# Deformable convolution on one core: chunks of consecutive window positions, with only the tokens that reach them

## The chip, the cores and the metric

One Trainium2 chip, one of its cores. The metric is the device time of one execution in microseconds; three runs of the kernel before are given with their median. The profile is of one more execution. Engine names: PE is the matrix engine (TensorE; its weight loads are listed apart, as PEld), DVE is VectorE, ACT is ScalarE, POOL is GpSimd, and SP is the engine from whose queue this kernel issues its transfers.

## The reference, cut to what matters

The network has four layers over eight images of 56 x 56 positions and 128 channels. Layers 0, 2 and 3 are of one kind, a deformable convolution (DCN) with a multilayer perceptron behind it; layer 1 is a state-space scan and isn't touched here. Of a DCN layer:

```python
xp = x @ w_in + b_in
h = gelu(batchnorm(depthwise_conv3x3(x)))
offset = (h @ w_off + b_off).reshape(N, H, W, GROUP, P, 2)
mask = softmax((h @ w_msk + b_msk).reshape(N, H, W, GROUP, P))
y = dcn_core(xp, offset, mask) @ w_out + b_out
x = x + gamma1 * layer_norm(y, ln1_g, ln1_b)
m = gelu(x @ w_fc1 + b_fc1) @ w_fc2 + b_fc2
x = x + gamma2 * layer_norm(m, ln2_g, ln2_b)
```

dcn_core takes, for every token, for each of 4 channel groups of 32 and each of 9 taps, a bilinear sample of xp at the tap's place plus its offset, and adds the 9 samples with the mask's weights. All is float32.

## The kernel before

**From gathering to matrix products.** The kernel doesn't gather. A block is 14 rows by 8 columns of an image: 112 tokens (TB). All samples of a token fall into a window of WY rows around it, and the windows of a block's tokens lie in one rectangle of 14 + WY - 1 rows, each PC positions wide. The weights of a token's 36 samples are added up into its own window, as one row of numbers per channel group. Shifted so that all 112 rows refer to the same rectangle, these rows are a matrix `sw` [112 tokens, 4 groups, SLEN positions]. The result of a group is then this matrix times the rectangle's rows of xp, `xw` [positions, 128 channels]. Row r of a block's tokens has nonzero weights in the rectangle's rows r to r + WY - 1 only; the rest of its row of `sw` is zeros.

**Chunks.** [...] the rectangle is cut into NJ chunks of KP positions. Stage 0 (layer 0): WY 14, PC 18, 4 chunks of 128. Stage 2: WY 12, PC 17, 4 of 112. Stage 3: WY 15, PC 21, 5 of 120. Before, chunk j holds the positions j, j + NJ, j + 2 NJ, ...: the positions are dealt out to the chunks in turn, so each chunk reaches over the whole rectangle.

**A block's work** (`sample`, lines 725 to 736, and `products`, lines 738 to 741). For each chunk: four PE transposes (line 732), one a group, turn the chunk's columns of `sw`, [112, KP] with a stride of NJ elements, into [KP, 112] in a PSUM bank `pt`; one ACT copy (line 734) brings the 4 x 112 columns to `st` in SBUF; four matrix products (line 741), one a group, with the chunk's rows of `xw` as the stationary operand (KP x 32), add [32, 112] into the block's columns of `yps`. Each float32 product is two instructions in the trace, a transpose is one. The products stand two chunks behind the transposes (`LAG`). A chunk's first product starts the sum, the last chunk's ends it.

**Loading.** `fetch` (lines 715 to 723) issues two transfers a block from SP's queue, two blocks ahead, into tiles with three buffers: `sw` from a table in DRAM to which `weigh` has stored the tokens' windows, and `xw` from the table that holds xp cut into strips. `windows` gives the second one's address pattern; before, partition p takes the NJ positions from p x NJ on, which lie side by side, so a partition's part is one contiguous piece of NJ x 512 bytes.

**The order around it** (`loop`, lines 826 to 875). Blocks run image by image, 4 block rows of 7 blocks: 224 a stage. Between the blocks' work the loop deals out, step by step, the tail of the block row before (output projection, two layer norms, the perceptron), the front of the next image (projection, depthwise convolution, offsets and masks) and `weigh`, which runs 6 blocks ahead (DVE adds each tap's patch into a window that POOL has cleared; ACT makes the bilinear weights). Each engine runs its instructions in the order that the framework's scheduler has written out; transfers leave SP's queue in theirs. Stores are collected and issued behind a fetch (`flush`).

Of the kernel before, what the change touches and what calls it, by code (L numbers as in the profile page):

```python
# [41 lines left out]
F32 = mybir.dt.float32  # L42
# [18 lines left out]
BR, BC = 14, 8  # L61
TB, NCB, NRB = BR * BC, W // BC, H // BR
# [12 lines left out]
class Geo:  # L75


    def __init__(self, y0, wy, x0, wx, kx, ky):
        self.Y0, self.WY, self.X0, self.WX = y0, wy, x0, wx

        self.PC, self.HR = BC + wx - 1, 14 * -(-(H + wy - 1) // 14)
        m = (BR + wy - 1) * self.PC
        self.NJ = -(-m // 128)
        self.KP = 8 * -(-m // self.NJ // 8)
        if self.KP % 16 and self.KP != 120:
            self.KP += 8
        self.SLEN = self.NJ * self.KP

        self.SA = G * self.SLEN
        self.WPAD = -(-(wy * self.PC + wx - kx) // 4) * 4  # L90


G, NP, CG = 4, 9, 32
# [363 lines left out]
class Dcn:  # L457
# [207 lines left out]
    def windows(self, i, c, rb=None):  # L665

        t, geo = self.table[i % 3], self.geo
        at = geo.HR * geo.PC * c
        if rb is None:
            return t[at : at + geo.HR * geo.PC].rearrange("(r x) c -> r (x c)", x=geo.PC)  # L670
        at += BR * rb * geo.PC
        return t[at : at + geo.SLEN].rearrange("(p j) c -> p (j c)", j=geo.NJ)

# [39 lines left out]
    def fetch(self, i, rb, q):  # L715

        nc, n, geo = self.nc, TB, self.geo
        sw = self.bp.tile([128, G, geo.SLEN], F32, name="sw", tag="sw")
        nc.sync.dma_start(out=sw[:n].rearrange("p g m -> p (g m)"), in_=self.slot(NRB * i + rb, q=q))
        xw = self.bp.tile([128, geo.NJ, C], F32, name="xw", tag="xw")  # L720
        last = nc.sync.dma_start(out=xw[: geo.KP].rearrange("p j c -> p (j c)"), in_=self.windows(i, q, rb))
        self.here[i, rb, q] = sw, xw
        return last

    def sample(self, i, rb, q, yps):

        nc, n, KP, NJ = self.nc, TB, self.geo.KP, self.geo.NJ
        sw, xw = self.here.pop((i, rb, q))
        for j in range(NJ):
            ps = self.pt.tile([128, 512], F32, name="pt", tag="pt")  # L730
            for g in range(G):
                last = nc.tensor.transpose(ps[:KP, n * g : n * (g + 1)], sw[:n, g, j::NJ], self.net.ident[:n, :n])  # L732
            st = self.bp.tile([128, G * n], F32, name="st", tag="st", bufs=4)
            nc.scalar.copy(st[:KP], ps[:KP, : G * n])  # L734
            self.behind.append(partial(self.products, yps, xw, st, j))
            self.catch_up(LAG, last)

    def products(self, yps, xw, st, j):
        n, KP = TB, self.geo.KP
        for g in range(G):  # L740
            self.nc.tensor.matmul(yps[CG * g : CG * (g + 1), :], lhsT=xw[:KP, j, CG * g : CG * (g + 1)], rhs=st[:KP, n * g : n * (g + 1)], start=j == 0, stop=j == self.geo.NJ - 1)  # L741

    def catch_up(self, lag, last=None):
        while len(self.behind) > lag:
# [692 lines left out]
```

## Time and profile before

| | |
|---|---|
| median of 3 runs | 19078.62 us (19069.39 to 19079.6) |
| profiled execution | 19113.06 us, span 19111.5 us |
| PE | busy 14938.0 us, 78% of the span |
| DVE | 15302.6 us, 80% |
| ACT | 11472.3 us, 60% |
| POOL | 11709.1 us, 61% |
| transposes, L732 | x11648, 2271.6 us busy, mean 327 ns |
| copies, L734 | x2912, 1516.3 us, 541 ns |
| products, L741 | x23296, 1357.6 us, 308 ns |
| granted PE clock | mean 0.833 |
| DMA, the three DCN loops | 0.84, 0.78 and 0.74 busy |

How to read it: the span's busy shares mix very different stages. The three DCN stages take about the first 2.3 ms and the last 5 ms; the scan layer with its long DVE and POOL instructions lies between them. A matrix instruction's length in the trace [...] overlaps with the next ones, so the distance from one start to the next tells more than the mean. PE's clock is granted in two values, half and full[...]. A line number is that of the kernel before.

### The profile page before, as it was taken

How to read it: one execution, taken by the hardware profiler on the slowest of the kernel's cores; microseconds unless marked ns; L12 is line 12 of the kernel's file. 1: busy time of each engine (PE TensorE's matmuls, PEld its weight loads, DVE VectorE, ACT ScalarE, POOL GpSimd, SP SyncE). 2: the span in 40 equal slices, each digit the busy share in tenths (PEclk: the TensorE clock that was granted, in tenths of full speed). 3: DMA queues.
4: the chain of work that ended last, by engine and by line, in shares of the span. 5: the costliest groups of instructions: out<-in, count | busy, mean ns of one | idle time of the engine just before them, and what ended most of it. 6: DMA issues, size and time to landing. Idle time of an engine off the chain costs nothing. (4 is left out here: it accounts for less than half of the span.)

```text
span 19111.5 us, 237768 instructions
## 1 busy us (share of the span) xinstructions
PE 14938.0 (78%) x80131; PEld 7162.2 (37%) x80131; DVE 15302.6 (80%) x18773; ACT 11472.3 (60%) x21363; POOL 11709.1 (61%) x6462
## 2 busy tenths in 40 slices
PE   5988877678778778778778778777667999588888
PEld 3666522122222222222222222222135666455555
DVE  6777468988988988988889889888957776677775
ACT  3666655566656556566556566656555666456565
POOL 1111069989989989988989989988951111111111
PEclk7888888889888888888888888888877888677777
DMA  8888633344443433344344443443326878577776
GB/s 240 230 222 228 185 127 139 138 142 143 141 143 140 144 141 140 141 142 144 138 143 142 143 143 138 146 144 130 138 88 187 214 211 207 154 205 203 195 205 173
DMA packets 981448, 3112.21 MB, mean 163 GB/s; under 512 B 76320, under 2 KB 518452, under 8 KB 912380
## 3 DMA queue, kind: packets, MB, share of 16 engines
q1 hardware_dynamic: 980204, 3096.75, 52.3%
q8 instruction: 644, 10.55, 0.2%
q14 instruction: 600, 4.92, 0.1%
HBM read 2395.38 MB, written 872.17 MB: 171 GB/s over the span
## 5 line engine op out<-in xcount | busy, mean ns | idle before, releaser
L1349 POOL TENSOR_TENSOR hc<-h,bc 128x784 f32<-128x784 f32 x4096 | 7568.1, 1872 | 1034.4 <-DVE h L1344 791.0
L1344 DVE TENSOR_TENSOR_SCAN h<-dA,st,u 128x784 f32<-128x784 f32 x3072 | 5577.7, 1837 | 392.0 <-ACT dA L1246 256.9
L1246 ACT ACTIVATE dA<-dt,v_A 128x784 f32<-128x784 f32 x4096 | 3741.2, 914 | 785.3 <-DVE h L1344 782.1
L1278 PE MATMUL acc<-hc,v_sum 128*32 128x392 f32 x16384 | 3422.7, 566 | 92.6 <-POOL hc L1349 92.1
L1256 DVE TENSOR_TENSOR u<-dtu,bc 128x784 f32<-128x784 f32 x3072 | 2883.1, 956 | 596.0 <-PE dtu L1240 468.9
L1240 PE MATMUL dtu<-dt,ident 128*128 128x392 f32 x4096 | 2103.4, 640 | 1342.2 <-issue 937.2
L732 PE MATMUL pt<-ident,sw 112*120 112x112 f32 (+2 forms) x11648 | 2271.6, 327 | 260.7 <-DMA sw<-skew 254.6
L734 ACT COPY st<-pt 120x448 f32<-120x448 f32 (+2 forms) x2912 | 1516.3, 541 | 1408.6 <-PE pt L732 1396.0
L700 POOL MEMSET win<- 128x1820 f32 (+2 forms) x384 | 631.5, 1647 | 2768.7 <-DMA skew<-win 2273.6
L1344 DVE TENSOR_TENSOR_SCAN h<-dA,st,up 128x784 f32<-128x784 f32 x1024 | 1878.8, 1835 | 258.9 <-POOL hc L1349 133.3
L732 PEld LDWEIGHTS pt<-ident,sw 112*120 112x120 f32 (+2 forms) x11648 | 1672.4, 204 | 852.4 <-issue 733.9
L1347 ACT COPY st<-h 128x1 f32<-128x1 f32 x3072 | 580.1, 189 | 2254.7 <-DVE h L1344 2244.6
L1252 POOL TENSOR_TENSOR up<-dt,bc 128x784 f32<-128x784 f32 x1024 | 1899.7, 1855 | 35.6 <-DVE h L1344 30.7
L1278 PEld LDWEIGHTS acc<-hc,v_sum 128*32 128x32 f32 x16384 | 804.4, 120 | 2617.4 <-issue 1702.9
L1240 PEld LDWEIGHTS dtu<-dt,ident 128*128 128x128 f32 x4096 | 858.7, 233 | 2417.8 <-issue 1481.9
L709 DVE TENSOR_TENSOR win<-win,patch 112x252 f32 (+2 forms) x3456 | 1558.2, 462 | 58.1 <-issue 17.3
L706 DVE TENSOR_TENSOR patch<-ay,hat 112x756 f32<-112x756 f32 (+2 forms) x1152 | 1213.2, 1065 | 488.5 <-POOL ay L697 488.4
L697 POOL TENSOR_TENSOR ay<-hat,om 112x756 f32<-112x756 f32 (+2 forms) x192 | 398.9, 2078 | 1950.8 <-ACT hat L693 1633.4
L741 PE MATMUL yps<-st,xw 120*32 120x112 f32 (+2 forms) x23296 | 1357.6, 308 | 133.8 <-ACT st L734 128.7
L1023 PE MATMUL misc<-xn,v_tap 128*128 128x448 f32 x2016 | 875.4, 579 | 120.3 <-ACT xn L1057 63.5
L1289 ACT COPY y<-acc 64x392 f32<-64x392 f32 x768 | 576.2, 750 | 460.4 <-PE acc L1278 450.4
L595 DVE SCALAR_TENSOR_TENSOR cv<-pad,w_col,cv 128x784 f32<-128x784 f32 x768 | 798.5, 1040 | 4.7
(158 smaller groups left out, 19403.2 us busy)
## 6 DMA issues: line engine op xcount, KB each, us to landing
dt<-dds SPq DMA_DIRECT2D x1024, 784.0 KB
bc<-rows SPq DMA_DIRECT2D x512, 784.0 KB
sw<-skew SPq DMA_DIRECT2D x224, 1050.0 KB
sw<-skew SPq DMA_DIRECT2D x224, 896.0 KB
dds<-dd SPq DMA_DIRECT2D x256, 784.0 KB
sw<-skew SPq DMA_DIRECT2D x224, 784.0 KB
skew<-win SPq DMA_DIRECT2D x128, 964.7 KB
skew<-win SPq DMA_DIRECT2D x128, 771.8 KB
```

What stands on the lines that cost most here:

```text
L706: nc.vector.tensor_mul(patch[:n], bcast(a, 3, KX), bcast(b, 2, KY))
L709: self.last_add = nc.vector.tensor_add(to, to, patch[:n, NCB * p : NCB * (p + 1)]).ins
L732: last = nc.tensor.transpose(ps[:KP, n * g : n * (g + 1)], sw[:n, g, j::NJ], self.net.ident[:n, :n])
L734: nc.scalar.copy(st[:KP], ps[:KP, : G * n])
L741: self.nc.tensor.matmul(yps[CG * g : CG * (g + 1), :], lhsT=xw[:KP, j, CG * g : CG * (g + 1)], rhs=st[:KP, n * g : n * (g + 1)], start=j = ...
L1240: last = nc.tensor.matmul(ps[:, b, :SH], lhsT=self.net.ident, rhs=s["dt", cg][:, 1, SH * b : SH * (b + 1)], start=True, stop=True)
L1246: nc.scalar.activation(da[:, :SC], s["dt", cg][:, 0], AF.Exp, scale=w["A"][:, k, NSG * cg + sg : NSG * cg + sg + 1])
L1252: nc.gpsimd.tensor_mul(u, s["dt", cg][:, 1], s["bc", sg][:, 0])
L1256: nc.vector.tensor_mul(halves[0], s["dtu", cg][:, :, :SH], halves[1])
L1278: nc.tensor.matmul(acc[r : r + TC, :SH], lhsT=w["sum"], rhs=hc[:, SH * b : SH * (b + 1)], start=False, stop=sg == NSG - 1)
L1344: nc.vector.tensor_tensor_scan(hh[:, ::step], dA[:, :SC][:, ::step], u[:, ::step], st[:, t : t + 1], ALU.mult, ALU.add)
L1349: nc.gpsimd.tensor_mul(hc, hh, s["bc", sg][:, 1])
```

## The change

Chunk j now holds the KP consecutive positions from j x KP on. Only some of the rectangle's rows fall into it, and so only tokens of some block rows have weights there. A new list `chunks` in the geometry gives for each chunk its number and the tokens t0 to t1 that can reach it; t0 is either 0 or 64. They are sorted so that a chunk with all 112 tokens comes first, since it starts the sum over all columns. In order, the chunks cover: stage 0 tokens 0 to 112, 0 to 112, 0 to 64 and 64 to 112; stage 2 0 to 112, 0 to 112, 0 to 56 and 64 to 112; stage 3 0 to 112 twice, 0 to 96, 0 to 48 and 64 to 112. Transposes, copy and products of a chunk work on these tokens alone. The transposes' source is now contiguous (no stride), and where a chunk has 64 tokens or fewer, they use half of PE's rows, the lower or the upper half. In `xw`, partition p now holds the positions p, KP + p, 2 KP + p, ..., so a partition's part comes in NJ pieces of 512 bytes. The numbers of instructions and of transfers stay as they are.

```diff
@@ class Geo
+        self.chunks = []
+        for j in range(self.NJ):
+            top, last = j * self.KP // self.PC, ((j + 1) * self.KP - 1) // self.PC
+            t0, t1 = BC * max(0, top - wy + 1), BC * min(BR, last + 1)
+            self.chunks.append((j, 64 if t0 >= 64 else 0, t1))
+        self.chunks.sort(key=lambda chunk: (chunk[1], -chunk[2]))
+        assert self.chunks[0][1:] == (0, TB)
@@ def windows
-        return t[at : at + geo.SLEN].rearrange("(p j) c -> p (j c)", j=geo.NJ)
+        return t[at : at + geo.SLEN].rearrange("(j p) c -> p j c", j=geo.NJ)
@@ def fetch
-        last = nc.sync.dma_start(out=xw[: geo.KP].rearrange("p j c -> p (j c)"), in_=self.windows(i, q, rb))
+        last = nc.sync.dma_start(out=xw[: geo.KP], in_=self.windows(i, q, rb))
@@ def sample
-        nc, n, KP, NJ = self.nc, TB, self.geo.KP, self.geo.NJ
+        nc, KP = self.nc, self.geo.KP
         sw, xw = self.here.pop((i, rb, q))
-        for j in range(NJ):
+        for at, (j, t0, t1) in enumerate(self.geo.chunks):
+            n = t1 - t0
             ps = self.pt.tile([128, 512], F32, name="pt", tag="pt")
             for g in range(G):
-                last = nc.tensor.transpose(ps[:KP, n * g : n * (g + 1)], sw[:n, g, j::NJ], self.net.ident[:n, :n])
-            st = self.bp.tile([128, G * n], F32, name="st", tag="st", bufs=4)
-            nc.scalar.copy(st[:KP], ps[:KP, : G * n])
-            self.behind.append(partial(self.products, yps, xw, st, j))
+                last = nc.tensor.transpose(ps[:KP, n * g : n * (g + 1)], sw[t0:t1, g, KP * j : KP * (j + 1)], self.net.ident[t0:t1, t0:t1])
+            st = self.bp.tile([128, G * TB], F32, name="st", tag="st", bufs=4)
+            nc.scalar.copy(st[:KP, : G * n], ps[:KP, : G * n])
+            self.behind.append(partial(self.products, yps, xw, st, at))
             self.catch_up(LAG, last)
@@ def products
-    def products(self, yps, xw, st, j):
-        n, KP = TB, self.geo.KP
+    def products(self, yps, xw, st, at):
+        KP = self.geo.KP
+        j, t0, t1 = self.geo.chunks[at]
+        n = t1 - t0
         for g in range(G):
-            self.nc.tensor.matmul(yps[CG * g : CG * (g + 1), :], lhsT=xw[:KP, j, CG * g : CG * (g + 1)], rhs=st[:KP, n * g : n * (g + 1)], start=j == 0, stop=j == self.geo.NJ - 1)
+            self.nc.tensor.matmul(yps[CG * g : CG * (g + 1), t0:t1], lhsT=xw[:KP, j, CG * g : CG * (g + 1)], rhs=st[:KP, n * g : n * (g + 1)], start=at == 0, stop=at == self.geo.NJ - 1)
```

## The prediction

> **What bounds the kernel now.** I read the sliced page first, to find where the changed code runs: the three deformable-convolution (DCN) stages, slices 0 to 4 and 30 to 39; the 12 ms between them are another layer, which the diff doesn't touch. Then each DCN loop as one window (stage 0, 2, 3 in turn; columns: window, length, then busy us and instructions of PE, PE's weight loads, DVE, ACT and POOL, granted PE clock, DMA share, GB/s), then who PE and the DMA queue wait for.
>
> ```profile
> 260.00:2260.00 2000.00, 1779.26 (x14710) 1242.62 (x14708) 1424.74 (x3120) 1285.19 (x2442) 361.30 (x204) 0.84 0.84 228
> 14480.00:16320.00 1840.00, 1695.86 (x14696) 1177.88 (x14694) 1262.37 (x3108) 1233.17 (x2381) 308.67 (x203) 0.88 0.78 207
> 16550.00:19075.00 2525.00, 2133.77 (x17360) 1432.22 (x17355) 1844.92 (x3123) 1529.92 (x2843) 428.58 (x203) 0.77 0.74 201
> ...
> SPq L721 <- PE yps L741: 676.4, 151, 22.0
> PE pt L732 <- DMA sw<-skew: 69.1, 33, 7.7
> ```
>
> PE is busy 89, 92 and 85% of the loops; DVE, ACT and POOL have more room. In stage 0 the queue that loads a block's data waits 676 us for PE to free a buffer, and PE waits only 69 us for that data. So PE sets the pace, with DMA close behind (0.84 in stage 0). Clocks of 0.84, 0.88 and 0.77, between the values 0.5 and 1.0 that the records hold, mean half clock for 32, 24 and 46% of the time.
>
> What PE does per chunk shows in the timeline (start, length, instruction, count): two chunks at full clock in stage 0, one at half clock in stage 2, and transposes of the same form whose source lies contiguous (L562, L776), at full clock.
>
> ```profile
> 1043.98 0.73 PE L732 MATMUL pt<-ident,sw 112*128 112x112 f32 x4
> 1044.64 0.40 PE L741 MATMUL yps<-st,xw 128*32 128x112 f32 x8
> 1044.97 0.73 PE L732 MATMUL pt<-ident,sw 112*128 112x112 f32 x4
> ...
> 14500.72 0.60 PE L741 MATMUL yps<-st,xw 112*32 112x112 f32 x8
> 14501.26 1.01 PE L732 MATMUL pt<-ident,sw 112*112 112x112 f32 x4
> 14502.20 0.60 PE L741 MATMUL yps<-st,xw 112*32 112x112 f32 x8
> ...
> 14510.52 0.68 PE L732 MATMUL pt<-ident,sw 112*112 112x112 f32 x4
> 14620.63 0.55 PE L562 MATMUL ps<-ident,xt 112*128 112x112 f32 x4
> 15138.04 0.60 PE L776 MATMUL ps<-ident,X 112*128 112x112 f32 x4 [0.27 <-DVE X L823]
> ```
>
> A chunk takes 0.99 us at full clock (1043.98 to 1044.97) and 1.48 at half. A block has 4, 4 and 5 chunks, 224 blocks a stage; 7080 product instructions in the first window, 32 a block, make 221 blocks in 2000 us: 9.05 us a block. The others likewise: 8.33 and 11.41.
>
> **Part 1, fewer columns.** From the geometry, chunks cover (112, 112, 64, 48), (112, 112, 56, 48) and (112, 112, 96, 48, 48) tokens instead of 112 each: 112, 120 and 144 columns less a block. The price of a column comes from start-to-start times in the trace: L783 with 448 columns starts every 376 ns at full clock, 747 at half: 0.84 and 1.67 ns. A token is streamed by 4 transposes one after another, and by 8 product instructions that run as 2 rounds of four side by side (starts 6 ns apart within a round, 100 between rounds): 6 column times, 5.0 and 10.0 ns. Per block: 0.56, 0.60, 0.72 us at full clock, 1.12, 1.20, 1.44 at half.
>
> [...] contiguous transposes (L776, 128 columns) start 96 ns apart, and their loads, when pulled ahead, as little as 57. [...]
>
> **Part 2, contiguous source.** Four transposes of strided `sw` take 0.73 us (128 positions), 0.68 (112); contiguous ones 0.60 with the switch ahead, 0.55 without. I take 0.13 a chunk in stage 0 and 0.08 in 2 and 3: 0.52, 0.32, 0.40 us a block. At half clock both forms start 187 ns apart: nothing.
>
> In the measured clock mix: stage 0 0.68x1.08 + 0.32x1.12 = 1.09 us; stage 2 0.76x0.92 + 0.24x1.20 = 0.99; stage 3 0.54x1.12 + 0.46x1.44 = 1.27. Times 224: 750 us of PE time.
>
> **Part 3, the 64-row mode.** Chunks of 64 tokens or fewer use transposes on half the rows. [...] 190 to 213 ns between a product and a transpose against 96 to 120 between two transposes. But every chunk already changes mode twice; the built instruction order has 11,592 changes against 11,424. 168 more at 0.1 us each: 17 us. No transpose on 64 rows is in this trace; bounds in the rivals.
>
> **Part 4, copies.** L734 takes 541 ns for 448 columns and L563's 336 take 438: 0.92 ns a column, so ACT loses about 0.4 us a block. It lies beside PE; without that cover (a product that waits for its copy, 36, 22 and 71 us in the loops) it is a small gain. Counted as nothing.
>
> **Part 5, the `xw` load.** Same bytes, but 512 B pieces instead of 2048 or 2560 B, 4 or 5 times as many. In the trace's packet records a 2048 B packet takes 130 ns in stage 0 (84 when undisturbed), 512 B packets in the middle layer 28. So 512 B costs 28, or by the same crowding 28x130/84 = 44; I take 36. Stage 0: 128 x 130 / 16 engines = 1.04 us a block becomes 512 x 36 / 16 = 1.15; stage 2 0.95 becomes 1.0, stage 3 1.11 becomes 1.35. Issuing costs little: `skew<-win` with 784 pieces takes 352 ns on SP, `xw` now 333. Waits are not added; behind this load stand the stores and the next `sw`, two blocks ahead of PE.
>
> **The sum.** DMA is busy 7.6, 6.5 and 8.4 us a block, then 7.7, 6.6, 8.6. The best half millisecond holds 0.85; I allow 0.90 (4 us windows reach 0.95): at least 8.55, 7.3 and 9.6 us. So stage 0 gains 0.5 of its 1.09; 2 and 3 are not capped. There I let three quarters through, since PE sits 8 and 15% idle on others and a less busy PE is granted less clock (0.88 at 92% busy, 0.77 at 85%): 0.74 and 0.95. (0.5 + 0.74 + 0.95) x 224 = 491, less 12 for the modes = 479. Profiled execution 19,113 (span 19,111.5): 18,634; the median of the runs lies 34 lower, so **18,600**.
>
> **Rivals.**
> - *PE alone sets it:* all 733 us come through: 18,346. For it: the queue's 676 us behind PE. Against: DMA would have to hold 0.97 in stage 0.
> - *Small pieces cost 55 ns:* DMA grows by 0.72, 0.59, 0.95 us a block; at 0.90 the blocks change by +0.15, -0.43, -0.95: 18,805.
> - *64-row transposes are no shorter:* only products, stride and copies gain, 372 us, some 70% through: 18,820. For it: no such row; against: L1001's 98 columns start 84 ns apart, 112 take 96.
> - *PE time turns into idle and lower clock:* no change, about 19,060.
> - *Slower, by the small pieces:* the place is `xw` at L721. At 80 ns a piece DMA grows by 1.5, 1.3, 1.9 us a block, and at 0.90 the blocks end at 10.1, 8.66, 11.4: +310 us, 19,389. It decides from about 67 ns, where the three stages cancel. Against it stand the 28 ns, and `skew<-win`'s 1008 B pieces at 55 ns in stage 0 itself.
>
> **Chances.** Forecast 0.49 (its own range 18,450 to 18,750), PE alone 0.12, 55 ns pieces 0.13, no shorter 0.08, no change 0.06, slower 0.12. Faster by over 0.2% (38 us, about what a measurement here can tell): 0.82; same 0.06; slower 0.12. The range 18,330 to 19,010 leaves out the slower case, no change, and a sliver below.
>
> **What would show it.** Right: L732's small forms start some 50 to 60 ns apart at full clock and 80 to 110 at half; four full ones take 0.60; a block takes 8.5, 7.6 and 10.4 us; 512 B packets 28 to 44 ns; DMA share up, to about 0.9 in stage 0. Wrong: small forms at 96 or 187 ns; PE waiting for `sw` or `xw` well over 69 us in stage 0; PE's clock falling to 0.7 with PE less busy and blocks as long as now. The middle layer should keep its length; if it doesn't, something that I haven't priced moved.

## The result: 0.3% faster, where 2.5% was forecast

| | before | after |
|---|---|---|
| median of 8 runs each | 19088.15 us (19069.39 to 19109.13) | 19028.97 us (19011.1 to 19048.64) |
| profiled execution | 19113.06 us | 19048.64 us |
| granted PE clock, mean | 0.833 | 0.805 |
| PE busy, whole span | 14938.0 us | 14638.0 us |

The ratio is 0.9966, 95% interval 0.9957 to 0.9976. The forecast was 18,600, its range 18,330 to 19,010.

**The profile after.** The three DCN loops as windows (window, length, busy us and instructions of PE, PE's weight loads, DVE, ACT and POOL, granted PE clock, DMA share, GB/s):

```profile
260.00:2220.00 1960.00, 1669.05 (x14566) 1135.37 (x14569) 1423.20 (x3092) 1189.44 (x2412) 365.01 (x203) 0.75 0.87 229
14460.00:16270.00 1810.00, 1620.88 (x14571) 1098.67 (x14564) 1262.82 (x3096) 1146.37 (x2352) 306.49 (x204) 0.78 0.81 211
16500.00:19010.00 2510.00, 2022.53 (x17540) 1364.21 (x17540) 1859.74 (x3143) 1431.99 (x2865) 433.67 (x206) 0.70 0.78 205
```

The clock stood at 0.84, 0.88 and 0.77 before; it is 0.75, 0.78 and 0.70 now. The page's clock row, in 40 slices, shows where: first before, then after.

```profile
PEclk7888888889888888888888888888877888677777
```

```profile
PEclk7777788889888888888888888888776777676677
```

Slices 1 to 4, 28, 30 to 33, 36 and 37 (counted from 0) go down by a tenth; from 5 to 27, most of which is the middle layer, the row is unchanged. That layer kept its length: from the last `yT` of stage 0 to the first of stage 2 it is 12,234 us before and 12,242 after. From one copy of `yT` to the next, a block takes 8.90, 8.23 and 11.22 us, against 8.99, 8.27 and 11.39 by the same measure before: 0.09 + 0.04 + 0.17 = 0.30 us, times 224 blocks 67 us. That is the whole difference between the two profiled executions (64 us).

The changed lines themselves did shrink, by the page's groups (busy us, mean ns, then idle time ahead of them and its releaser):

```profile
L741 PE MATMUL pt<-ident,sw 112*128 112x112 f32 (+8 forms) x11648 | 1901.3, 300 | 354.3 <-DMA sw<-skew 348.4
L743 ACT COPY st<-pt 128x448 f32<-128x448 f32 (+6 forms) x2912 | 1236.7, 443 | 1359.5 <-PE pt L741 1312.7
L752 PE MATMUL yps<-st,xw 120*32 120x48 f32 (+8 forms) x23296 | 1211.8, 294 | 213.0 <-ACT st L743 197.8
```

Transposes lost 2271.6 - 1901.3 = 370 us and products 1357.6 - 1211.8 = 146, together 516. But PE as a whole lost 300 only. Its other instructions, the same 45,187 in both kernels, are busy 179 us longer, all of it in the three loops (their records added up by themselves: 2551 us before, 2731 after); the rest of the difference is overlap. And of these 300 the span got 64; what remains became idle time. Waits in stage 0 after (us in total, times, longest), the queue's and PE's:

```profile
SPq L540 <- DVE win L717: 464.6, 76, 13.9
SPq L729 <- PE pt L741: 406.6, 102, 17.8
SPq L729 <- PE yps L752: 214.8, 62, 10.5
...
PE pt L741 <- DMA sw<-skew: 93.3, 44, 6.7
PE yps L752 <- ACT st L743: 63.6, 34, 6.7
```

The first line before:

```profile
SPq L532 <- DVE win L709: 384.1, 74, 11.6
```

At the load of `xw` the queue still waits for PE to free buffers (406.6 + 214.8 = 621 us; before 676.4 + 37.0 = 713 by the same view). But the first line, which the prediction left out, is as long: before it can issue the stores of `weigh`, the queue waits for DVE to finish the windows. In stage 3 that is its longest wait in both kernels (722.9 us before, 801.0 after). So PE paces the blocks, but not alone; DVE stands close behind it. PE itself waits more for `sw` (93 us, 69 before) and for copies (64, 33 before by the same view).

One place of stage 3 shows both the gain and its price (timeline of PE after; start, length, instruction, count, idle before):

```profile
16728.79 0.43 PE L741 MATMUL pt<-ident,sw 48*120 48x48 f32 x4
...
16729.84 0.37 PE L752 MATMUL yps<-st,xw 120*32 120x96 f32 x8
16733.77 0.57 PE L741 MATMUL pt<-ident,sw 112*120 112x112 f32 x4 [3.55 <-DMA sw<-skew]
...
16734.58 1.00 PE L741 MATMUL pt<-ident,sw 112*120 112x112 f32 x4
16735.52 0.39 PE L752 MATMUL yps<-st,xw 120*32 120x48 f32 x8
...
16737.20 0.63 PE L741 MATMUL pt<-ident,sw 48*120 48x48 f32 x4
```

At 16728.79 a chunk of 48 tokens needs 0.43 us for its transposes. Then PE waits 3.55 us for `sw`, finds full clock for one more chunk's transposes (the clock record falls to half at 16734.2), and from 16734.58 on everything takes its half-clock length: the same 48 tokens 0.63 us.

### The profile page after: what moved, and what is told of

It reads as the page before. It is cut to its first block, busy times and chain, and to the rows that moved or that the text cites. A ratio compares the mean times of both kernels' runs of the same rounds, so it can differ in the third digit from the quotient of the medians.

```text
span 19047.1 us, 237826 instructions
## 1 busy us (share of the span) xinstructions
PE 14638.0 (77%) x80131; PEld 6918.2 (36%) x80131; DVE 15315.5 (80%) x18773; ACT 11199.2 (59%) x21363; POOL 11707.3 (61%) x6462
## 5 line engine op out<-in xcount | busy, mean ns | idle before, releaser
L741 PE MATMUL pt<-ident,sw 112*128 112x112 f32 (+8 forms) x11648 | 1901.3, 300 | 354.3 <-DMA sw<-skew 348.4
L743 ACT COPY st<-pt 128x448 f32<-128x448 f32 (+6 forms) x2912 | 1236.7, 443 | 1359.5 <-PE pt L741 1312.7
L741 PEld LDWEIGHTS pt<-ident,sw 112*128 112x128 f32 (+8 forms) x11648 | 1329.5, 170 | 879.1 <-issue 647.4
L752 PE MATMUL yps<-st,xw 120*32 120x48 f32 (+8 forms) x23296 | 1211.8, 294 | 213.0 <-ACT st L743 197.8
L794 PE MATMUL ps<-xT,w_fc 128*128 128x448 f32 (+1 forms) x1536 | 794.0, 651 | 114.8 <-ACT xT L789 86.9
```

The source lines that it names most:

```text
L743: nc.scalar.copy(st[:KP, : G * n], ps[:KP, : G * n])
L752: self.nc.tensor.matmul(yps[CG * g : CG * (g + 1), t0:t1], lhsT=xw[:KP, j, CG * g : CG * (g + 1)], rhs=st[:KP, n * g : n * (g + 1)], start ...
```

## The experiments

The expectations speak of three theories. The clock theory (C): PE paces, at a clock that is granted by what its own work does. W: DVE's `weigh` paces. D: loads or DVE hold the blocks. Ratios are to the kernel before on the same chip, with 95% intervals; block times and clocks of the loops are of the profiled execution, measured from the first copy of `yT` to the last (before, this gives 0.85 for stage 0 where the window above gave 0.84).

| run | median us | ratio | clock | block us, stages 0 / 2 / 3 | loop clock |
|---|---|---|---|---|---|
| before | 19088.15 | 1 | .833 | 8.99 / 8.27 / 11.39 | .85 / .88 / .77 |
| after | 19028.97 | .9966 [.9957, .9976] | .805 | 8.90 / 8.23 / 11.22 | .76 / .78 / .70 |
| e1 all tokens | 19026.57 | .9947 [.9929, .9965] | .831 | 8.84 / 8.16 / 11.29 | .84 / .87 / .77 |
| f1 transposes on all rows | 18957.46 | .9921 [.9904, .9937] | .822 | 8.85 / 8.09 / 11.18 | .80 / .84 / .75 |
| e4 half of `sw` loaded | 19024.28 | .9952 [.9935, .9968] | .808 | 9.03 / 8.14 / 11.23 | .74 / .78 / .72 |
| e5 before, a third of `weigh` | 18760.03 | .9813 [.9797, .983] | .843 | 8.77 / 8.20 / 10.29 | .85 / .88 / .83 |
| e6 after, a third of `weigh` | 18802.87 | .9836 [.9819, .9852] | .808 | 8.69 / 8.24 / 10.50 | .75 / .77 / .71 |
| e8 without chunks of 64 or fewer | 18771.42 | .9819 [.9802, .9835] | .802 | 8.45 / 7.83 / 10.85 | .74 / .77 / .69 |
| e12 before, filler | 18853.86 | .9865 [.9849, .9882] | .870 | 8.68 / 8.23 / 10.67 | .95 / .96 / .91 |
| e7 all tokens, filler | 18828.43 | .9852 [.9835, .9868] | .870 | 8.59 / 8.11 / 10.69 | .94 / .96 / .90 |
| e11 all tokens, filler of 32 columns | 18856.12 | .9862 [.9845, .9878] | .870 | 8.62 / 8.18 / 10.77 | .95 / .97 / .90 |
| f6 all tokens, filler on 32 rows | 19607.83 | 1.0256 [1.024, 1.0272] | .829 | 9.28 / 9.52 / 12.05 | .87 / .81 / .77 |
| f4 all tokens, two fillers | 18965.43 | .9933 [.9915, .9951] | .879 | 8.87 / 8.73 / 10.45 | .96 / .97 / .96 |
| e2 after, filler on full chunks | 18985.76 | .9928 [.991, .9945] | .823 | 8.77 / 8.19 / 11.17 | .82 / .84 / .74 |
| e3 the same, 32 columns | 19029.8 | .9958 [.9943, .9973] | .824 | 8.81 / 8.29 / 11.18 | .81 / .84 / .75 |
| e9 after, filler on every chunk | 19008.46 | .9943 [.9927, .996] | .846 | 8.82 / 8.26 / 11.17 | .87 / .89 / .82 |
| e10 after, two fillers on full chunks | 18922.92 | .9899 [.9882, .9915] | .845 | 8.75 / 8.06 / 10.98 | .87 / .91 / .81 |
| f2 all rows, filler | 18793.18 | .9838 [.982, .9856] | .862 | 8.52 / 7.99 / 10.78 | .92 / .96 / .88 |
| f3 all rows, two fillers | 18873.32 | .9879 [.9863, .9896] | .878 | 8.65 / 8.53 / 10.41 | .96 / .97 / .95 |
| f5 all rows, fillers by stage | 18736.69 | .9803 [.9789, .9816] | .870 | 8.62 / 8.00 / 10.42 | .92 / .96 / .95 |

### Loads and DVE: not what took the gain back

e4 loads two of the four groups of `sw` and uses each twice:

```diff
-        return bass.AP(tensor=t.tensor, offset=t.offset + q * TB * geo.SA, ap=[[BC * geo.SA - geo.PC, BR], [geo.SA - 1, BC], [1, G * geo.SLEN]])
+        return bass.AP(tensor=t.tensor, offset=t.offset + q * TB * geo.SA, ap=[[BC * geo.SA - geo.PC, BR], [geo.SA - 1, BC], [1, G // 2 * geo.SLEN]])
-        nc.sync.dma_start(out=sw[:n].rearrange("p g m -> p (g m)"), in_=self.slot(NRB * i + rb, q=q))
+        nc.sync.dma_start(out=sw[:n, : G // 2].rearrange("p g m -> p (g m)"), in_=self.slot(NRB * i + rb, q=q))
-                last = nc.tensor.transpose(ps[:KP, n * g : n * (g + 1)], sw[t0:t1, g, KP * j : KP * (j + 1)], self.net.ident[t0:t1, t0:t1])
+                last = nc.tensor.transpose(ps[:KP, n * g : n * (g + 1)], sw[t0:t1, g // 2, KP * j : KP * (j + 1)], self.net.ident[t0:t1, t0:t1])
```

> The changed kernel with half of sw loaded (two of the four groups; groups 2 and 3 are computed with the weights of groups 0 and 1's planes, so the output differs): DMA loses about 1.8 us of its 7.7 a block, PE's work is the same. Theory C: the time falls by at most 150 us, what PE waited for sw in the loops (93 + 33 + 142 us). Theory D with the loads as the bound: by 400 us or more.

The DMA share fell from 0.87, 0.80 and 0.78 to 0.62, 0.58 and 0.56, and the time hardly moved: 0.9952 against 0.9966, overlapping intervals. So bandwidth is not the limit, not in stage 0 either, where the forecast capped the gain at a DMA share of 0.90. The waits only move: in stage 3, PE waits 37 us for `sw` instead of 142, and 241 us instead of 86 for `X`, which DVE makes.

e5 and e6 cut `weigh` to the first three of nine taps in the kernel before and in the changed one:

```diff
-                for p0 in range(0, NP, PP):
+                for p0 in range(0, PP, PP):
```

> The kernel before with a third of weigh's patches: only the first 3 of 9 taps of each group are multiplied and added into the windows (the other taps' weights are left out, so the output differs). DVE loses about 3.9 us a block in stage 3 and 2.5 to 3 in the others; PE, the loads and ACT keep their work. Theory W (weigh on DVE, with the ACT and POOL work and the stores that go with it, paces the blocks beside PE, and the time taken from PE became idle time): this one is 300 us or more faster than the kernel before, and the lightened changed kernel gains another 250 to 500 us on top. Theory C (PE paces the blocks at a clock that its use of the array sets): this one is within 200 us of the kernel before.

> The same cut of weigh (taps 3 to 8 left out, so the output differs) in the changed kernel. What counts is its distance to the lightened kernel before. Theory W: 250 to 500 us, what was forecast for the change, since now only PE is left to pace. Theory C: the distance stays what it is without the cut, 60 to 100 us, because PE is granted a lower clock all the same.

Both gain over 1.5%, mostly in stage 3. So DVE's part matters to the whole: e5's 359 us are more than the 200 that the clock theory allowed, and are what theory W asked for. In this the clock theory was wrong. But if DVE hid the change's gain, taking two thirds of `weigh` away would let it out: W asked for the changed kernel to end 250 to 500 us sooner, the clock theory 60 to 100. It ends 43 us *later* than the old one (18,803 against 18,760), with DVE busy about half of the loops and the queue's wait for DVE's windows in stage 3 down to 15 us in e5 and 14 in e6. Stage 3 in the windows view of e6:

```profile
16435.00:18750.00 2315.00, 1962.96 (x17270) 1326.97 (x17265) 1155.09 (x2122) 1409.40 (x2807) 407.39 (x201) 0.71 0.84 218
```

DVE is busy 1155 of 2315 us; the clock is still 0.71, against 0.83 in the old kernel with the same cut. DVE is a limit of its own, but W falls as the explanation of the lost gain; the clock stays.

### The change taken apart

e1 keeps consecutive positions and contiguous transposes, with all 112 tokens in every chunk. f1 narrows copy and products to the chunk's tokens, but not the transposes:

```diff
@@ e1
-            self.chunks.append((j, 64 if t0 >= 64 else 0, t1))
+            self.chunks.append((j, 0, TB))
@@ f1
-                last = nc.tensor.transpose(ps[:KP, n * g : n * (g + 1)], sw[t0:t1, g, KP * j : KP * (j + 1)], self.net.ident[t0:t1, t0:t1])
+                last = nc.tensor.transpose(ps[:KP, TB * g : TB * (g + 1)], sw[:TB, g, KP * j : KP * (j + 1)], self.net.ident[:TB, :TB])
-            nc.scalar.copy(st[:KP, : G * n], ps[:KP, : G * n])
+            nc.scalar.copy(st[:KP, : G * n].rearrange("p (g t) -> p g t", g=G), ps[:KP, : G * TB].rearrange("p (g t) -> p g t", g=G)[:, :, t0:t1])
```

> Chunks of consecutive positions as in the changed kernel, but all 112 tokens in every chunk: contiguous transposes and the 512 B pieces of xw alone. Theory C (PE still sets the pace; its clock is granted by how much of the array the work fills, and the smaller operations lost it): nothing gets smaller, so the clock stays near that of before (0.84, 0.88, 0.77 in the three loops, mean 0.83), the transposes gain at full clock only, and the time is 18,900 to 19,020, not worse than the changed kernel although it does all the work of the dropped tokens. Theory D (loads or DVE hold the blocks, and PE's clock falls only because PE idles): the time is the changed kernel's within 40 us, and PE is busier. A plain count of PE work would say 19,113 - 300 + 450, some 350 us slower than a kernel without those tokens.

> The changed kernel with one thing undone: every chunk's transposes take all 112 tokens again (contiguous source, 112 rows, 112 columns); copy and products keep to the tokens t0 to t1. Clock theory (PE paces[...]): [...] the clock comes back to that of the kernel with all tokens: about 0.83, loops near 0.84/0.87/0.77; the time is at or below that kernel's 0.9947 of before: 0.988 to 0.994. Rival (any streamed column counts alike, so the narrower products take as much clock as the narrower transposes): clock at most 0.82, time 0.995 to 0.998.

In order of the steps: contiguous 0.9947, narrower copies and products too 0.9921 (these two intervals overlap), narrower transposes too (the change) 0.9966. The last step takes work off PE and makes the kernel 0.45% slower than without it; here the intervals lie apart. e1's 19,027 us are just outside its range, which ended at 19,020. f1's loops in the windows view:

```profile
267.00:2218.00 1951.00, 1698.27 (x14623) 1156.95 (x14626) 1423.22 (x3088) 1197.14 (x2421) 348.33 (x203) 0.80 0.87 232
14455.00:16239.00 1784.00, 1619.90 (x14625) 1109.34 (x14623) 1271.32 (x3087) 1142.37 (x2361) 291.97 (x203) 0.84 0.82 212
16485.00:18949.00 2464.00, 2018.05 (x17263) 1351.04 (x17264) 1838.91 (x3104) 1416.25 (x2828) 428.88 (x203) 0.75 0.79 206
```

PE is as long busy as in the changed kernel (1698, 1620, 2018 us against 1669, 1621, 2023), although it streams 112 columns in every transpose: the clock, 0.80, 0.84 and 0.75, pays for them. The time came where the clock theory put it; the clock itself came out a little under its figure (0.822 for 0.83; e1 has 0.831), so narrowing the products seems to cost some.

e8 goes the other way and leaves the chunks of 64 tokens or fewer out altogether, 6 of 13 over the three stages (the line that ends the sum with the last chunk is adapted, not shown):

```diff
+        self.chunks = [chunk for chunk in self.chunks if chunk[2] - chunk[1] > 64]
```

> The changed kernel without the chunks of 64 tokens or fewer: their transposes, copies and products are left out (the output differs), 2 of 4, 2 of 4 and 2 of 5 chunks; every load stays. PE loses some further 1.5 to 1.9 us a block at full clock. Theory W: no more than 100 us faster than the changed kernel, PE's clock near or under 0.75. Theory C: some 100 to 250 us faster, since full chunks keep the clock up (0.80 or more). PE's work as such: 700 us or more faster.

PE's busy share drops to 73, 77 and 71%, and the time by 1.5% only against the changed kernel. The clock stays about where the changed kernel has it (0.74, 0.77, 0.69), under the 0.80 that the clock theory asked for. So full chunks alone don't keep the clock up, and most of this saving went another way: PE is busy for 920 us less than in the changed kernel (14,638 to 13,718), the profiled execution is shorter by 276, and PE waits 253 us for `sw` in stage 0 and 335 in stage 3 where the changed kernel has 93 and 142. What holds the blocks in e8 was not tried.

### More work, more clock

The direct test of a clock that depends on PE's work is useless work. A *filler* is one bf16 product of 512 columns into the PSUM bank that the chunk's transposes then overwrite:

```diff
+        self.fill = self.const("fill", [128, 512], BF16)
+        nc.vector.memset(self.fill, 1.0)
@@ def sample
             ps = self.pt.tile([128, 512], F32, name="pt", tag="pt")
+            nc.tensor.matmul(ps[:128], lhsT=self.fill[:, :128], rhs=self.fill, start=True, stop=True)
             for g in range(G):
```

> The kernel before (strided chunks, all tokens, xw in whole pieces) with the wide matmul ahead of every chunk. Theory C: the clock rises to about 0.87 or more here too, and the kernel gets 0.5 to 1.3% faster although it does more work on PE; the rest of the way to the all-token kernel with filler is the contiguous source, which counts at full clock only. PE's work as such: 300 us slower.

The kernel before, with 2912 such products added and nothing else changed, is 1.35% faster, which is four times what the change gives. PE's busy time over the whole span stays the same, 14,941 us for 14,938: the fillers take no more than the rest gives back by running faster. Its loops:

```profile
266.00:2180.00 1914.00, 1787.13 (x15512) 1270.68 (x15511) 1437.90 (x3090) 1272.40 (x2422) 343.18 (x203) 0.95 0.86 237
14401.00:16215.00 1814.00, 1732.78 (x15511) 1213.83 (x15503) 1280.36 (x3089) 1229.70 (x2363) 296.92 (x203) 0.96 0.79 209
16459.00:18811.00 2352.00, 2068.62 (x18368) 1425.47 (x18367) 1840.99 (x3101) 1518.18 (x2828) 423.76 (x203) 0.91 0.80 215
```

The clock goes from 0.84, 0.88, 0.77 to 0.95, 0.96, 0.91; nearly all of the gain is in stages 0 and 3, where it was lowest. The same ahead of every chunk of e1 (e7), and with the filler's stationary part cut to 32 columns (e11):

> All 112 tokens in every consecutive chunk, and the wide bf16 matmul ahead of every chunk (896, 896 and 1120 of them): more PE work than in any kernel so far, and the fullest use of the array. Theory C: the clock rises above 0.85, and the time stays at or under that of the all-token kernel (-80 to +40 us). Theory W: within 60 us of it as well, with PE busier. If PE's work as such sets the pace: 400 us slower.

> All 112 tokens in every consecutive chunk, with the narrow (32 columns of the array) matmul ahead of every chunk, in place of the wide one: the same streaming time, a quarter of the array. If the gate answers to the filled part of the array: the mean clock is well under the 0.87 of the wide one (0.82 to 0.85), and the time at or over that of the all-token kernel without filler (0.993 to 1.005 of before). If it answers to busy time alone: as with the wide one, 0.87 and 0.985.

0.9852 and 0.9862 at the same clock: whether the filler fills 128 of the array's columns or 32 made no difference to it (0.870 both), and with that fell the earlier idea that the filled area counts. On the changed kernel the filler was tried ahead of full chunks only (e2; e3 with 32 columns), twice there (e10), and ahead of every chunk (e9):

> The changed kernel with one bf16 matmul more ahead of each full chunk, 128 rows x 128 columns, 512 streamed columns, whose result is overwritten: 1344 of them, 0.21 us each at full clock and 0.43 at half, 290 to 570 us of PE work added. Theory C: the mean clock rises from 0.805 to 0.83 or more and the time stays or falls (-150 to +50 us). Theory D: the time stays within 40 us whatever the clock. If PE sets the pace and the clock doesn't answer to the array's use, the time rises by 250 to 500 us.

> The same added matmul with 32 columns of the array instead of 128: the same time on PE, a quarter of the array. Theory C: the clock hardly moves (0.79 to 0.82) and the time rises by 150 to 400 us over the changed kernel. Theory D: within 60 us of the changed kernel, like the wide one.

> The changed kernel with the wide bf16 matmul ahead of every chunk, the small ones too. Theory C (PE's clock answers to how much of the array the work fills; the change lost its gain to the clock): the clock rises to 0.85 or more, as with all tokens and the same filler (0.87), and the dropped tokens now pay: 60 to 250 us faster than that kernel, 0.972 to 0.982 of the kernel before. If the all-token kernel with fillers was faster for another reason than the clock, or the 64-row mode keeps the clock down: no faster than it (0.985 or more).

> The changed kernel with two wide matmuls ahead of each full chunk and none ahead of the small ones: about as much filler as one ahead of every chunk, without a further change of mode. Theory C: the clock lies above the 0.823 of one filler per full chunk, the time 30 to 150 us under it. PE's added work as such: 150 us or more over it.

All raise the clock, but e9 stays at 0.9943, far from what I expected: with the small chunks' transposes the clock comes back to 0.87, 0.89 and 0.82 only, and from a filler on all rows to a 48-token transpose it is 320 ns, against 226 to a full one. e10 has nearly as many fillers (2688 for 2912) and the same clock (0.845 for 0.846), all ahead of full chunks, and is faster: 0.9899. Two clocks missed: e2's 0.823 is under the expected 0.83, and e3's 0.824 over the 0.79 to 0.82 that went with the filled area. f2 puts the transposes back on all rows:

> The kernel of the run with transposes on all rows, plus one 512-column filler matmul ahead of each chunk. Clock theory: clock about 0.87, as with all tokens and a filler, and the shorter products and copies now count: 0.980 to 0.985, just below 0.9852. Rival (the fillers' place and order, not the rows, made the difference between the filler with all tokens, 0.9852, and the filler ahead of each small chunk, 0.9943): stays near 0.994.

```profile
264.00:2142.00 1878.00, 1713.82 (x15491) 1155.78 (x15487) 1431.32 (x3090) 1191.27 (x2421) 342.69 (x203) 0.92 0.89 241
14376.00:16138.00 1762.00, 1649.31 (x15515) 1114.99 (x15513) 1265.51 (x3089) 1136.76 (x2363) 314.11 (x203) 0.96 0.84 215
16384.00:18760.00 2376.00, 2024.76 (x18370) 1335.93 (x18367) 1838.92 (x3102) 1416.80 (x2828) 426.97 (x203) 0.88 0.81 213
```

0.9838, inside the 0.980 to 0.985 that the clock theory gave; the rival had it at 0.994. With the clock back, PE's waits shrink as well (stage 0 of f2):

```profile
PE pt L746 <- DMA sw<-skew: 40.2, 28, 4.7
...
PE yps L757 <- ACT st L748: 20.0, 26, 1.8
```

40 and 20 us where the changed kernel has 93 and 64. So at least part of PE's added idle time in the changed kernel goes with the low clock and is no second cause.

Two fillers, with narrow (f3) and with all tokens (f4), and the count chosen by stage (f5: one in stages 0 and 2, two in stage 3):

> Transposes on all rows, two 512-column fillers ahead of each chunk. Clock theory: the clock is nearly full in the loops (over 0.95 in all three, about 0.89 over all), and PE's second filler, 0.21 us at full clock, eats what the rest of half clock gives back: 0.981 to 0.988. Rival (the gain of fillers isn't the clock): as with one filler plus 0.85 us of PE a block, 0.990 or more.

> All tokens in every consecutive chunk, two 512-column fillers ahead of each chunk. Clock theory: clock nearly full in the loops, about 0.89 over all, 0.982 to 0.990; by its distance from the kernel with transposes on all rows and two fillers one reads what the narrower copies and products are worth at nearly full clock (my guess 0.002). Rival: 0.990 or more.

> Transposes on all rows, narrow copies and products; one 512-column filler ahead of each chunk in stages 0 and 2, two in stage 3. Clock theory: PE paces in every stage, so each stage keeps the block time that it had with that number of fillers (8.52, 7.99 and 10.41 us): 18,793 less 0.37 us x 224 = 18,710, ratio 0.9794, within 0.977 to 0.982. Rival (the gain in stage 3 with two fillers came from how the stages hang together, not from that stage's clock): stays at 0.9838.

Two fillers bring all loops to 0.95 or more. There PE is simply too long: in stage 2, busy 97%, f3's blocks take 8.53 us against f2's 7.99. f4's 0.9933 missed my range on the slow side. The difference f4 to f3, 0.0054, is what narrower copies and products are worth at nearly full clock, more than the 0.002 I guessed. Stage 3 still gains from the second filler (10.41 for 10.78), and f5, which gives it there alone, is the fastest kernel of this study: 18,736.69 us, 0.9803 [0.9789, 0.9816].

### The filler on 32 rows

f6 is e7 with the filler contracting over 32 rows instead of 128: as many columns, as long a stream.

```diff
-            nc.tensor.matmul(ps[:128], lhsT=self.fill[:, :128], rhs=self.fill, start=True, stop=True)
+            nc.tensor.matmul(ps[:128], lhsT=self.fill[:32, :128], rhs=self.fill[:32], start=True, stop=True)
```

> All tokens in every consecutive chunk, one filler of 512 columns ahead of each chunk, as long as the one that gave 0.9852 at a clock of 0.87, but contracting over 32 rows in place of 128. Clock theory with rows as the weight: [...] the clock stays near that without filler (0.831): 0.83 to 0.85 over all, and PE pays 0.21 us a chunk at full clock, twice that at half: 0.996 to 1.015. Rival (streaming time counts whatever the rows): clock 0.87, ratio 0.985 to 0.989.

```profile
275.00:2320.00 2045.00, 1949.98 (x15478) 1182.48 (x15478) 1433.92 (x3088) 1274.08 (x2419) 338.11 (x202) 0.87 0.83 221
14555.00:16654.00 2099.00, 2047.07 (x15515) 1207.80 (x15513) 1278.28 (x3088) 1249.08 (x2363) 291.73 (x203) 0.81 0.70 180
16910.00:19568.00 2658.00, 2464.36 (x18383) 1425.56 (x18379) 1835.56 (x3090) 1526.11 (x2829) 413.11 (x203) 0.77 0.73 190
```

PE is busy 95, 98 and 93%, more than in any other run here except those with two fillers, and its clock over all is as without filler (0.829; 0.831 in e1; by loop 0.87, 0.81 and 0.77 for e1's 0.84, 0.87 and 0.77), where e7's filler on all rows has 0.870. So more busy time alone brought no more clock here: the same 512 columns raised it over 128 rows and not over 32. The time missed my range on the slow side. The filler on 32 rows also costs PE time: 315 ns from filler to transpose instead of 226 (534 for 401 at half clock). That is 13 x 0.089 to 0.133 us x 224 = 259 to 387 us of the 772 that lie between f6 and e7 (0.0404 x 19,110); the rest is put down to the clock, and wasn't measured by itself.

The clock records of the before and after kernels also give the share of a loop that stood at half clock: 31% of stage 0 before and 49% now, 24 and 44% of stage 2, 46 and 60% of stage 3. Which property of PE's work sets the clock at a given moment was not shown; these runs compare whole loops.

## Why the prediction was wrong

- **What bounds.** PE was named, and that holds in part: with half of `sw` loaded (e4) the time hardly moves, and with e12's useless PE work the kernel gets faster by clock alone. DVE was said to have room, but e5, with less of it, gains 1.9%. And half of PE's bound was read as a constant: the mix of half and full clock stood in the table as if it belonged to the stage. It moved with PE's own work: 0.833 before, 0.805 after the change, 0.870 with e12's fillers.
- **Part 1, fewer columns.** The prices nearly held: transposes of 48 to 64 tokens start 55 to 64 ns apart at full clock and 93 to 108 at half (forecast 50 to 60, 80 to 110). With 112, 120 and 128 positions in a chunk, 48 tokens start 94, 100 and 107 ns apart at half clock. At both clocks 48 tokens take as long as 56 or 64 with the same number of positions (at full clock 55 and 57 ns with 112, 63 and 64 with 128), so the smallest chunks save a little less than their tokens were priced at. By the changed kernel's own start-to-start times parts 1 and 2 come to about 720 us in the clock mix of before, for 750.
- **Part 2, contiguous source.** Four full transposes take 0.55 to 0.60 us, as forecast. Alone (e1, clock nearly unchanged) it takes 176 us of PE's busy time (14,938 to 14,762), where the full-clock shares priced 182 (0.35, 0.24 and 0.22 us a block); 90 us of it reach the median.
- **Part 3, the 64-row mode.** Still 190 ns at full clock, 325 at half, from a full product to the next transposes; the count of such steps rose by little. Small, as said. That the clock would fall with the smaller transposes (0.822 in f1, 0.805 with them) was not thought of.
- **Part 4, copies.** Priced at nothing behind PE. ACT lost 280 us (1516.3 to 1236.7 by line). What copies alone are worth wasn't tried; at nearly full clock copies and products together are worth 0.54% (f4 against f3).
- **Part 5, small pieces.** 38, 40 and 37 ns a piece, where 36 was taken; 1.22, 1.10 and 1.37 us a block for 1.15, 1.0 and 1.35. The DMA total came out at 7.70, 6.61 and 8.75 us for 7.7, 6.6 and 8.6. The rivals at 55 and 80 ns are out; no cost here.
- **The sum: the step that failed.** "In the measured clock mix: stage 0 0.68x1.08 + 0.32x1.12" and its two fellows gave 750 us, at the clock of before. The mix became 0.51 to 0.49, 0.56 to 0.44 and 0.40 to 0.60. In PE's busy time 300 us are left of the 750. The term left out is what the lower clock costs the work that stays, and it comes to about 410 us: a block's chunks in the changed kernel take 2.96, 2.87 and 3.66 us at full clock and 4.84, 4.67 and 6.00 at half, and 18, 20 and 14% more of the time is at half, which makes some 230 us in 224 blocks a stage; the instructions that nobody touched make the other 179. About 30 us were priced too high in part 1. Of the 300, 236 turned into idle time. The discount in the sum stood for that: the cap in stage 0 and "three quarters" in the others take off 0.59 + 0.25 + 0.32 = 1.16 us a block, 260 us. So the idle time was about as large as forecast, though in stage 0 by luck, since the DMA share that was to cap it is not the limit (e4); and the clock's 410 us come on top. The sentence that a less busy PE is granted less clock was in the prediction, but as a reason for a quarter's discount, not as a term with a size.
- **The rivals.** "PE time turns into idle and lower clock: no change, about 19,060", given 6 in 100, is close to what happened: 31 us off, with a small gain that is clear of the noise. In hindsight it deserved the most weight: 13 to 14% of PE's busy time was to be saved (1.09 of 8.05 us a block in stage 0), in stages where the clock already stood at half for a quarter to a half of the time, and the three loops before had the lower clock where PE was less busy.
- **What would show it.** The last sign named for "wrong" is the one seen: clock falling to 0.7 with PE less busy and blocks about as long as before. PE's waits for `sw` in stage 0 rose from 69 to 93 us only.

## What to carry to other kernels

A mean PE clock between 0.5 and 1 in the profile was a result here, not a constant (0.805 after the change, 0.833 before, 0.870 with e12's fillers): before pricing a saving in PE work, ask whether the clock will stay without that work, and price what stays once more at a lower one. With PE pacing at such a clock, cutting rows and columns from its transposes cost more than it saved (f1 0.9921, the change 0.9966; which of the two cuts costs more was not tried apart), and a useless product on all rows paid: 1.35% on the unchanged kernel. The way to both gains was to narrow what cost little clock (products and copies, 0.831 to 0.822 from e1 to f1), leave the transposes on all rows, and add filler by stage until PE itself was the limit.

## What the runs showed of the hardware that was not expected

- The granted clock moved with PE's work. A filler on all rows ahead of every chunk raised its mean from 0.833 to 0.870 (before to e12) and from 0.831 to 0.870 (e1 to e7). With 32 columns in place of 128 it was 0.870 too (e11), over 32 rows 0.829 (f6). Transposes on a chunk's tokens alone took it from 0.822 to 0.805 (f1 to the change).
- In the timeline of stage 3 above, the clock record falls to half at 16734.2, after PE's wait of 3.55 us; four 48-token transposes then take 0.63 us instead of 0.43.
- From a filler on all rows and columns to a full transpose it is 226 ns (e7), from one on 32 rows 315 (f6), from one with 32 columns 310 to 320 (e11's timeline); from a filler on all rows to a 48-token transpose 320 (e9).
- The small transposes' distance went with the number of positions in the chunk, not with the tokens: 55, 59 and 63 ns at full clock for 112, 120 and 128 positions, 94, 100 and 107 at half, all with 48 tokens; 56 tokens took 57 ns with 112 positions, 64 tokens 64 with 128.
- Pieces of 512 B took a median of 28 to 31 ns (mean 37 to 40) in the changed kernel where pieces of 2048 B took 107 to 116 (mean 130 to 136) in stages 0 and 2 before: a quarter of the size took a bit over a quarter of the time (28 of 107 ns, 31 of 116).
